# A graph-convolution kernel: zero rows behind h written first, x's other rows loaded in eight pieces on SyncE's queue, clearings begun five groups later

## The chip, the cores and the metric

The kernel runs on one core of one Trainium2 chip. The metric is the device time in microseconds of one execution; of several executions the median is taken.

## The reference: what is computed

A pre-normalised message-passing layer over 12,500 nodes and 400,000 edges, all in float32, with feature width 128 and 20 radial features per edge. The edges come sorted by `dst`.

```python
h = jnp.maximum(_layernorm(x, axis=-1), 0.0)           # [12500, 128]
h = h @ W_in2f.T
Wij = smu(f_ij @ W_f1.T + b_f1) @ W_f2.T + b_f2        # [400000, 128]
Wij = Wij * rcut_ij[:, None]
x_ij = h[idx_j] * Wij                                  # idx_j is dst (sorted)
agg = jax.ops.segment_sum(x_ij, idx_i, num_segments=h.shape[0])   # idx_i is src (any order)
out = smu(agg @ W_o1.T + b_o1) @ W_o2.T + b_o2
x = x + out
```

`smu` is a gelu-like bend with an erf in it.

## The kernel before, in words

**Tiles, groups, passes.** 128 edges are a tile, 4 tiles a group (512 edges), 8 tiles a super-tile (`SUP`, two groups). The 3,125 tiles are cut into nine passes (`PARTS`, called epochs in the code); the first has 59 super-tiles, that is 118 groups. For each group TensorE, ScalarE and VectorE make the messages: `hide` (L517) and `weigh` (L567) are the two filter products, `bend` (L525) and `smooth` (L533) the bend between them, `gather` (L548) takes the rows of h with a one-hot product, `take` (L556) copies them, `mix` (L577) multiplies, `turn` (L587) transposes back, and `send` writes the message tile `ms`: the row index within the bin by VectorE (L594), the four scaled copies by ScalarE (L597). Then GpSimd stores the four tiles with one indirect DMA each (L600) into DRAM buckets `buf{k}` of the pass, one bucket for each of the 98 bins of 128 nodes. Where a row goes is found by counting: `bins` (L438, L449, L452), `count` (L465, L466), `read` (L495), `number` (L504). While pass k makes messages, the buckets of pass k-1 are loaded (`fetch`, L631) and summed with one-hot products (`choose` L642, `add` L655). The fetch of a pass's buckets waits until all its stores have landed.

**Buckets must be cleared.** The tail of every bucket, from a guaranteed fill on, is set to zero by DMAs from the `zero` tile (`clear`, L167; 387 KB for two bins), issued by SyncE. For pass 0 they run in groups 0 to 37, spread evenly, and the constant `BY` (44 groups) is the point up to which the messages surely stay below the cleared region; later stores may wait for the clearings. From group `BY` on the clearings of pass 1 are issued, to the end of the pass.

**h and its windows.** The rows of h are needed by edges whose `dst` they are, and `dst` is sorted, so the first pass needs only the rows of the first 4 bins (`HEAD`). They are made before the loop; the other 94 bins are made during the first pass and stored in `h_dram` (L214). Each super-tile loads one window of 128 rows of `h_dram` at a row number that is read from SBUF (`window`, L415 and L416). Because that address is known only at run time, such a load is ordered against every write of `h_dram`, and every write against the loads before it. `N + WIN` rows exist; the ones behind the last bin must be zero. `zeroed` writes them (L731 to L733).

**The order of the work is written out by hand.** For TensorE, VectorE, ScalarE and SyncE the instruction order is the program's order; each works through its own in turn. The main loop over the groups (L776) first issues the loads of a later super-tile (`load`, L405 for the radial features, L407 for the relative indices, L416 for the window), then clearings, then the group's work. Three times in a group it calls `step()`: after `turn` and `send` of this group (the first slot), after `mix` of the next group (the second slot), and at the end (the third slot). `step()` takes from a list of side steps, `others()`, at an even pace: a step is taken while `taken_steps * 318 < slot * COUNT`, so at 276 steps nearly every slot takes one. The list is:

- the limits of chunk 0 and `zeroed`;
- for each of six further chunks of 512 tiles (`head_of`): `fetched` (SyncE asks for `dst` and `src`, 256 KB each, L301 and L302), `based` (VectorE's first use of `dst`, L305 to L307), `spread` (TensorE, L312), `lowered` (VectorE, L316), `turned` (TensorE, L321), `written` (ScalarE L327, then SyncE's store to `rel_dram`, L328), `binned`, `placed`, `limits`; after each of these nine one `stats` of a bin of x (L180, L181);
- the remaining `stats`, two in a step;
- `deviations`, and then 24 units of `rows_of_h` of six steps each: `normed` (VectorE, L191), `turned` (TensorE, L197), `cut` (ScalarE, L200), `product` (TensorE, L205), `first_part` (L208, L209), `other_parts` (L212, L213 and the store L214);
- `output_bias`.

**x.** x lives in the tile that later holds `agg`. Its first four bins are loaded at the start on ScalarE's queue. `late_loads` (L374) asks for the others on GpSimd's queue: three DMAs of 31 bins (L381, 1984 KB each) and one for the last bin (L382), then the rest of the edge weights (L384, 1306.5 KB) and small things. Small writes by VectorE (L376, L379) hold these DMAs back until that point.

**hs.** One tile `hs` (bufs=1) takes the three bf16 parts of h before they are stored, and serves as the buffer of `written` in the chunks after the first.

Of the kernel before, what the change touches and what calls it, by code (L numbers as in the profile page):

```python
# [9 lines left out]
F32 = mybir.dt.float32  # L10
# [9 lines left out]
P = 128  # L20
# [19 lines left out]
def gnn_kernel(  # L40
# [129 lines left out]


    HEAD = 4
    BY = 44
    x_sb = agg.rearrange("p (b d) -> p b d", d=D)
    mv = const.tile([P, NB, 2], F32, name="mv")
    rstd = const.tile([P, NB], F32, name="rstd")
# [84 lines left out]
    with tc.tile_pool(name="ld", bufs=4) as ld, \  # L261
# [14 lines left out]
        def fill(i):  # L276
            nc.vector.memset(fbufs[i], 1.0)

        hs = edge.tile([P, GRP, 3, D], BF, name="hs", bufs=1)
        early = eps_of[0][1] + 3  # L280

        def bank(name):
# [2 lines left out]
        def head_of(c):  # L285


            a, n = c * CH, min(CH, NT - c * CH)
            s0, m = a // SUP, (n + SUP - 1) // SUP
            rw = rowp.tile([P, ROWS, ROW], F32, name="rw").rearrange("p q r -> p (q r)")  # L290
            di, si, rel = rw[:, 0:n].bitcast(I32), rw[:, CH:CH + n].bitcast(I32), rw[:, 2 * CH:2 * CH + n]
            if c:
                rb = hs[:, :, 0, :]
            else:
                rb = edge.tile([P, SUP * P], BF, name="oh", bufs=3)[:, :CH].rearrange("p (j e) -> p j e", e=P)
            base_f = edge.tile([1, CH // SUP], F32, name="base_f")
            cells = [(j * P, min(P, n - j * P)) for j in range((n + P - 1) // P)]
            kept = [None]

            def fetched():  # L300
                nc.sync.dma_start(di, dst_col[:, a:a + n])  # L301
                nc.sync.dma_start(si, src_col[:, a:a + n])  # L302

            def based():
                nc.vector.tensor_copy(base_i[:, s0:s0 + m], di[0:1, 0:n:SUP])  # L305
                nc.vector.tensor_copy(base_f[:, :m], base_i[:, s0:s0 + m])
                nc.vector.tensor_copy(rel, di)  # L307

            def spread():
                pb = kept[0] = bank("pb")  # L310
                flat = pb.rearrange("p j e -> p (j e)")[:, :m * SUP].rearrange("p (s t) -> p s t", t=SUP)
                nc.tensor.matmul(flat, ones1, base_f[:, :m].unsqueeze(2).to_broadcast([1, m, SUP]),  # L312
                                 start=True, stop=True)

            def lowered():
                nc.vector.tensor_sub(rel, rel, kept[0].rearrange("p j e -> p (j e)")[:, :n])  # L316

            def turned():
                pd = kept[0] = bank("pd")
                for j, (o, w) in enumerate(cells):  # L320
                    nc.tensor.transpose(pd[:w, j, :], rel[:, o:o + w], ident)  # L321

            def written():
                w = cells[-1][1]
                whole = len(cells) - (w < P)
                if whole:
                    nc.scalar.activation(rb[:, :whole], kept[0][:, :whole], AF.Copy)  # L327
                    nc.sync.dma_start(rel_dram[0, a * P:(a + whole * P) * P].rearrange("(c t e) -> t c e", t=P, e=P),  # L328
                                      rb[:, :whole])
                if w < P:  # L330
                    nc.scalar.activation(rb[:w, whole], kept[0][:w, whole], AF.Copy)
                    nc.sync.dma_start(rel_dram[0, (a + whole * P) * P:(a + n) * P].rearrange("(t e) -> t e", e=P),
                                      rb[:w, whole])

            def limits():
                nc.vector.tensor_reduce(lh[:, 0, c:c + 1], rel, op=ALU.min, axis=AX.X)
                nc.vector.tensor_reduce(lh[:, 1, c:c + 1], rel, op=ALU.max, axis=AX.X)

            def bounded():
                most = edge.tile([1, 1], F32, name="most")  # L340
                nc.vector.tensor_reduce(most, base_f[:, :early], op=ALU.max, axis=AX.X)
                nc.vector.tensor_scalar(bad[0:1, 2:3], most, float(HEAD * P - WIN), None, op0=ALU.is_gt)
                nc.vector.tensor_scalar(base_i[:, :early], base_f[:, :early], float(HEAD * P - WIN), None, op0=ALU.min)

            def binned():
                nc.vector.tensor_scalar(di, si, 7, None, op0=ALU.arith_shift_right)
                nc.vector.tensor_copy(hi_b[:, a:a + n], di)

            def placed():
                nc.vector.tensor_scalar(di, si, P - 1, None, op0=ALU.bitwise_and)  # L350
                nc.vector.tensor_copy(lo_b[:, a:a + n], di)

            return dict(fetched=fetched, based=based, spread=spread, lowered=lowered, turned=turned, written=written,
                        limits=limits, bounded=bounded, binned=binned, placed=placed)
# [9 lines left out]
        nc.scalar.dma_start(w_f2, w_f2_t)  # L364
        nc.scalar.dma_start(b2, b_f2.rearrange("o p -> p o"))
        nc.scalar.dma_start(w_sb[:, 0:CH], w_col[:, 0:CH])
        for i in range(NF):
            fill(i)
        nc.vector.memset(zero, 0.0)
# [4 lines left out]
        def late_loads():  # L374

            nc.vector.memset(x_sb[:, NB - 1, :], 0.0)  # L376
            parts_of_x = chunks(NB - 1 - HEAD, 31)
            for a, n in parts_of_x:
                nc.vector.memset(x_sb[:, HEAD + a, 0:1], 0.0)  # L379
            for a, n in parts_of_x:  # L380
                nc.gpsimd.dma_start(x_sb[:, HEAD + a:HEAD + a + n, :], bin_rows(x, HEAD + a, n))  # L381
            nc.gpsimd.dma_start(x_sb[:LASTB, NB - 1, :], x[(NB - 1) * P:N, :])  # L382
            nc.vector.memset(w_sb[:, CH:CH + 1], 0.0)
            nc.gpsimd.dma_start(w_sb[:, CH:NT], w_col[:, CH:NT])  # L384
            nc.gpsimd.dma_start(w_o1, w_o1_t)
            nc.gpsimd.dma_start(w_o2, w_o2_t)
            nc.gpsimd.dma_start(b1, b_o1.rearrange("o p -> p o"))
            nc.gpsimd.dma_start(b2row, b_f2)
            nc.gpsimd.dma_start(bo2, b_o2.to_broadcast([P, P]))
# [305 lines left out]
            stats(edge, b)  # L695
        deviations(0, HEAD)
        rw = rowp.tile([P, ROWS, ROW], F32, name="rw")
        for step in rows_of_h(0, HEAD, *[rw[:, j * GRP:(j + 1) * GRP, 0:P] for j in range(3)], hs, bank):
            step()
        for s in range(3):  # L700
            window(s)
# [25 lines left out]
        cleared = at_first = done = 0  # L727
        work = []

        def zeroed():  # L730
            zr = edge.tile([P, 3 * D], BF, name="zr", bufs=1)  # L731
            nc.vector.memset(zr, 0.0)
            nc.sync.dma_start(h_dram[NB * P:N + WIN, :], zr[:N + WIN - NB * P, :])  # L733

        def output_bias():

            nc.vector.tensor_scalar(w_o2, w_o2, GC, None, op0=ALU.mult)
# [3 lines left out]
            nc.tensor.matmul(pb1, b1w, w_o2, start=True, stop=True)  # L741
            nc.vector.tensor_add(bo2, bo2, pb1)

        def others():
            yield one["limits"]
            yield zeroed
            left = list(range(HEAD, NB))
            for c in range(1, NC):
                it = head_of(c)
                for name in ("fetched", "based", "spread", "lowered", "turned", "written", "binned", "placed", "limits"):  # L750
                    yield it[name]
                    if left:
                        yield lambda b=left.pop(0): stats(edge, b)
            while left:
                two, left = left[:2], left[2:]
                yield lambda two=two: [stats(edge, b) for b in two]
            yield lambda: deviations(HEAD, NB)
            for b, n in chunks(NB - HEAD, GRP):
                rw = rowp.tile([P, ROWS, ROW], F32, name="rw")
                four = [rw[:, j * GRP:(j + 1) * GRP, 0:P] for j in range(3)]  # L760
                yield from rows_of_h(HEAD + b, n, *four, hs, bank)
            yield output_bias

        COUNT = 2 + 18 * (NC - 1) + (NB - HEAD - 9 * (NC - 1) + 1) // 2 + 1 + 6 * -(-(NB - HEAD) // GRP) + 1
        h_steps = others()
        taken_steps = slot = 0

        def step():

            nonlocal taken_steps, slot  # L770
            slot += 1
            while taken_steps < COUNT and taken_steps * 3 * (eps_of[0][1] * PER - 12) < slot * COUNT:
                next(h_steps)()
                taken_steps += 1

        for g in range(NG):  # L776
# [7 lines left out]
                cleared = 0  # L784
            if g < BY:

                while at_first < min(len(cleans) - 1, -(-(g + 1) * (len(cleans) - 1) // (BY - 6))):
                    apart(clear(0, at_first, nc.sync), "filled", "cleared")
                    at_first += 1
            elif k + 1 < EPOCHS:  # L790
# [34 lines left out]
            bins(g + 3)  # L825
            parts(k - 1, hi)
            step()
            assert k == 0 or taken_steps == COUNT and next(h_steps, None) is None
        k = EPOCHS - 1
        begin(k)  # L830
        choose(k, order_of[k][0])
# [222 lines left out]
```

## Time and profile before

| What | us |
|---|---|
| median of 3 runs (lowest, highest) | 4170.57 (4166.96, 4171.32) |
| profiled execution, device time | 4170.47 |
| its span, first to last instruction | 4168.6 |
| first indirect store begins | 32.87 |
| last store of the first pass begins (store 472 of 3125) | 668.62 |
| last indirect store begins | 4057.5 |

The profiled execution's device time lies 1.9 us above its span. The profile's page gives, for each engine, its busy time, and for groups of instructions the mean duration and the idle time of the engine just before them, with what ended most of it. In the timeline a row is: start in us, duration in us, engine, line, operation, output<-inputs, and in brackets the idle time before it with its releaser. An engine written with a q (SPq, POOLq) is the sequencer that issues DMAs. In the list of windows, each engine's busy time is followed by its instruction count in brackets; then come TensorE's granted clock (1.00 is full), the mean busy share of the 16 DMA engines, and GB/s.

### The profile page before, as it was taken

What the parts mean: (1) busy time and instruction counts of PE and PEld (TensorE: products, weight loads), DVE (VectorE), ACT (ScalarE), POOL (GpSimd) and SP (SyncE); (2) the same over time, 40 slices, a digit from 0 to 9 for tenths busy, and PEclk for the clock granted to TensorE, in tenths of its full rate; (3) what the DMA queues carried; (4) which work ended last, traced back from release to release, by engine and by line L of the source; (5) the groups of instructions that cost most, each with busy time, mean ns of one, the idle gap of its engine ahead of it and who ended that gap; (6) DMA issues with size and microseconds to landing.
All of it is one profiled execution on the core that took longest, in us unless ns stands there. A gap on an engine that the chain in (4) does not pass through costs nothing.

```text
span 4168.6 us, 74614 instructions
## 1 busy us (share of the span) xinstructions
PE 3724.3 (89%) x18497; PEld 2310.5 (55%) x18794; DVE 3202.9 (77%) x8556; ACT 2823.1 (68%) x11054; POOL 3055.0 (73%) x3169
## 2 busy tenths in 40 slices
PE   6877888999997999979999979999899899899898
PEld 2333434655554655545655546666566566556567
DVE  6886767877776877768877768888688788788777
ACT  5776777776766777657777657777677667677651
POOL 4777767777777777777777777777777777777762
PEclk9999999999999999999999999999999999999999
DMA  8955565766656766647666747777699699788667
GB/s 232 226 149 167 175 169 177 215 202 193 201 165 190 214 203 199 199 142 217 209 202 196 200 150 216 212 212 206 180 231 232 172 250 253 211 224 223 172 186 233
DMA packets 510408, 834.71 MB, mean 200 GB/s; under 512 B 84499, under 2 KB 322852, under 8 KB 509838
## 3 DMA queue, kind: packets, MB, share of 16 engines
q1 hardware_dynamic: 393900, 608.10, 53.0%
q0 software_dynamic: 101872, 214.27, 16.7%
q10 hardware_dynamic: 14194, 7.46, 0.6%
q8 instruction: 152, 2.49, 0.3%
q14 instruction: 290, 2.38, 0.2%
HBM read 456.16 MB, written 373.36 MB: 199 GB/s over the span
## 4 chain that ended last, share of the span: by engine, by line
PE 55%; DVE 20%; DMA 14%; ACT 7%; issue 3%; POOL 1%; DVEq 0%; SPq 0%; POOLq 0%; ACTq 0%
PE pw L567 13%; PE pg L655 13%; DMA buf<-ms,ix 12%; PE pu L517 10%; PE ph L548 8%; PE pt L587 6%; DVE se L642 5%; DVE mt L577 4%; DVE sm L533 3%; ACT ge L525 2%; ACT ms L597 2%; ACT jk L495 2%; DVE co L452 1%; DVE po L438 1%; DVE agg L668 1%
## 5 line engine op out<-in xcount | busy, mean ns | idle before, releaser
L600 POOL DMA_INDIRECT buf<-ms,ix x3125 | 3013.1, 964 | 1018.3 <-issue 264.5
L655 PEld LDWEIGHTS pg<-se,rw 128*128 128x128 f32 x8036 | 1088.8, 192 | 153.0 <-issue 14.8
L597 ACT ACTIVATE ms<-pt,w_sb 128x128 f32<-128x128 f32 x3125 | 902.5, 391 | 332.5 <-PE pt L587 181.8
L655 PE MATMUL pg<-se,rw 128*128 128x128 f32 x8036 | 1110.3, 276 | 7.8 <-DVE se L642 7.8
L495 ACT ACTIVATE jk<-pc,nbig 128x98 f32<-128x98 f32 x3125 | 1024.5, 350 | 2.7 <-PE pc L466 2.0
L567 PE MATMUL pw<-sm,w_f 128*128 128x512 f32 x1564 | 885.5, 649 | 41.5 <-DVE sm L533 36.2
L525 ACT ACTIVATE ge<-pu 128x512 f32<-128x512 f32 x782 | 467.9, 598 | 569.2 <-PE pu L517 546.4
L577 DVE SCALAR_TENSOR_TENSOR mt<-pw,b,hg 128x512 f32<-128x512 f32 x782 | 583.0, 745 | 346.8 <-ACT hg L556 345.9
L517 PE MATMUL pu<-f,w_f 128*128 128x512 f32 x1564 | 814.3, 603 | 5.4 <-DVE sm L533 5.4
L587 PE MATMUL pt<-ident,mt 128*128 128x128 f32 x3125 | 494.5, 281 | 293.7 <-DVE mt L577 290.3
L533 DVE SCALAR_TENSOR_TENSOR sm<-pu,ge 128x512 f32<-128x512 f32 x782 | 535.2, 684 | 215.3 <-ACT ge L525 206.4
L642 DVE TENSOR_TENSOR se<-irow_ps,rw 128x1536 f32<-128x1536 f32 (+1 forms) x345 | 587.5, 1703 | 146.9 <-DMA rw<-buf 127.5
L556 ACT ACTIVATE hg<-ph 128x512 f32<-128x512 f32 x782 | 468.7, 599 | 325.5 <-PE ph L548 323.5
L495 ACT ACTIVATION_READ_ACCUMULATOR jk<-pc,nbig 128x1 f32 x3125 | 674.3, 216 | 0.0
L548 PE MATMUL ph<-oh,hw 128*128 128x512 bf16 (+1 forms) x2049 | 631.7, 387 | 16.6 <-issue 0.7
L587 PEld LDWEIGHTS pt<-ident,mt 128*128 128x128 f32 x3125 | 353.3, 142 | 383.4 <-DVE mt L577 375.4
L452 DVE TENSOR_TENSOR co<-co,po 128x98 f16<-128x98 f16 x2353 | 501.8, 213 | 81.1
L548 PEld LDWEIGHTS <-hw 128*128 128x128 bf16 x2346 | 233.0, 99 | 555.3 <-issue 455.9
L438 DVE TENSOR_TENSOR po<-irow_ps,hi_b 128x392 f16<-128x392 f32 x782 | 433.3, 554 | 0.0
L567 PEld LDWEIGHTS pw<-sm,w_f 128*128 128x128 f32 x1564 | 238.0, 191 | 172.8 <-DVE sm L533 163.7
L517 PEld LDWEIGHTS pu<-f,w_f 128*128 128x128 f32 x1564 | 254.3, 196 | 29.6 <-DVE sm L533 7.0
L465 PE MATMUL pc<-co,ones_h 128*128 128x392 f16 x782 | 258.0, 330 | 1.0 <-ACT ms L597 1.0
(122 smaller groups left out, 1708.6 us busy)
## 6 DMA issues: line engine op xcount, KB each, us to landing
rw<-buf SPq DMA_DIRECT2D x292, 774.0 KB
rbc<-rel_dram SPq DMA_DIRECT2D x390, 256.0 KB
buf<-zero SPq DMA_DIRECT2D x243, 387.0 KB
buf<-ms,ix POOLq DMA_INDIRECT x3125
buf<-zero SPq DMA_DIRECT2D x193, 258.0 KB
hw<-h_dram SPq DMA_DIRECT2D x391, 96.0 KB
rw<-buf SPq DMA_DIRECT2D x49, 645.0 KB
f<-in_f_t SPq DMA_DIRECT2D x390, 80.0 KB
```

The costliest lines, as they stand in the source:

```text
L495: nc.scalar.activation(jk, pc[:, j], AF.Relu, bias=nbig, accum_out=sl[:, j:j + 1])
L517: nc.tensor.matmul(pu[:, :n], w_f1, loaded[g // PER][0][:, o:o + n], start=True, stop=True)
L525: nc.scalar.activation(ge[:, :n], units_of[g][:, :n], AF.Gelu, scale=ZS)
L533: nc.vector.scalar_tensor_tensor(sm[:, :n], units_of.pop(g)[:, :n], LIN, hidden[g][:, :n], op0=ALU.mult, op1=ALU.add)
L548: nc.tensor.matmul(ph[:, :n], hw[:, q * D:(q + 1) * D], oh[:, o:o + n], start=(q == 0), stop=(q == 2))
L567: nc.tensor.matmul(pw[:, :n], w_f2, hidden.pop(g)[:, :n], start=True, stop=True)
L577: nc.vector.scalar_tensor_tensor(mt[:, :n], pws.pop(g)[:, :n], b2, rows_of.pop(g)[:, :n], op0=ALU.add, op1=ALU.mult)
L587: nc.tensor.transpose(pt[:, j, :], mt[:, j * P:(j + 1) * P], ident)
L597: nc.scalar.activation(ms[:, j, 0:P], pt[:, j], AF.Copy, scale=w_sb[:, t + j:t + j + 1])
L600: i = nc.gpsimd.indirect_dma_start(out=bufs[k][:, :], out_offset=bass.IndirectOffsetOnAxis(ap=ix[:, j:j + 1], axis=0), in_=ms[:, j, :], in ...
L642: nc.vector.tensor_tensor(se[:, :m], irow_ps.unsqueeze(1).to_broadcast([P, m, P]), rows_in[c][:, :m, P:P + 1].to_broadcast([P, m, P]), op= ...
L655: nc.tensor.matmul(pgs[0][:, g, :], rows_in[c][:, o, 0:P], sel[c][:, o, :], start=(q == 0), stop=(q == Q[k] - 1))
```

## The change

Four edits:

1. The zero rows behind h are written at the very start: the memset of `zr` stands ahead of VectorE's first fills, and the DMA goes on ScalarE's queue, behind its first loads. The step `zeroed` is gone.
2. x's other rows leave `late_loads` (with the small writes that held them back) and become eight pieces of 12 bins (786 KB, the last 10 bins) on SyncE's queue. They are side steps: one right after the limits of chunk 0, one ahead of each of the six chunks, and the last after them. Chunk 1 has no `stats` between its steps any more; the others have them as before, and what remains is taken in pairs.
3. The clearings of pass 0 begin in group 6 instead of group 0, at the same rate (48 in 38 groups), and `BY` is 50 instead of 44, which also moves the start of pass 1's clearings.
4. `hs` becomes a tile taken anew for each use from a pool of two buffers. The side steps are a list instead of a generator; `COUNT` becomes 279.

```diff
-    BY = 44
+    BY = 50
...
-        hs = edge.tile([P, GRP, 3, D], BF, name="hs", bufs=1)
+        def parts_tile():
+            return edge.tile([P, GRP, 3, D], BF, name="hs")
+
...
-                rb = hs[:, :, 0, :]
+                rb = parts_tile()[:, :, 0, :]
...
         nc.scalar.dma_start(w_sb[:, 0:CH], w_col[:, 0:CH])
+        zr = edge.tile([P, 3 * D], BF, name="zr", bufs=1)
+        nc.vector.memset(zr, 0.0)
+        nc.scalar.dma_start(h_dram[NB * P:N + WIN, :], zr[:N + WIN - NB * P, :])
         for i in range(NF):
             fill(i)
...
             nc.vector.memset(x_sb[:, NB - 1, :], 0.0)
-            parts_of_x = chunks(NB - 1 - HEAD, 31)
-            for a, n in parts_of_x:
-                nc.vector.memset(x_sb[:, HEAD + a, 0:1], 0.0)
-            for a, n in parts_of_x:
-                nc.gpsimd.dma_start(x_sb[:, HEAD + a:HEAD + a + n, :], bin_rows(x, HEAD + a, n))
-            nc.gpsimd.dma_start(x_sb[:LASTB, NB - 1, :], x[(NB - 1) * P:N, :])
...
-        def zeroed():
-            zr = edge.tile([P, 3 * D], BF, name="zr", bufs=1)
-            nc.vector.memset(zr, 0.0)
-            nc.sync.dma_start(h_dram[NB * P:N + WIN, :], zr[:N + WIN - NB * P, :])
...
+        def old_piece(a, n):
+            for b, m in chunks(n, n if a + n < NB else n - 1):
+                if a + b < NB - 1:
+                    nc.sync.dma_start(x_sb[:, a + b:a + b + m, :], bin_rows(x, a + b, m))
+                else:
+                    nc.sync.dma_start(x_sb[:LASTB, NB - 1, :], x[(NB - 1) * P:N, :])
...
+        PIECE = 12
+        loads = [lambda a=a, n=n: old_piece(HEAD + a, n) for a, n in chunks(NB - HEAD, PIECE)]
+        single = [lambda b=b: stats(edge, b) for b in range(HEAD, NB)]
+        steps = [one["limits"], loads.pop(0)]
+        for c in range(1, NC):
+            mine = named(lambda c=c: head_of(c),
+                         ("fetched", "based", "spread", "lowered", "turned", "written", "binned", "placed", "limits"))
+            if loads:
+                steps.append(loads.pop(0))
+            for f in mine:
+                steps.append(f)
+                if c > 1:
+                    steps.append(single.pop(0))
+        steps += loads
+        for i in range(0, len(single), 2):
+            steps.append(lambda two=single[i:i + 2]: [f() for f in two])
+        steps.append(lambda: deviations(HEAD, NB))
+        units_of_rows = [named(lambda b=b, n=n: rows_unit(HEAD + b, n), range(6)) for b, n in chunks(NB - HEAD, GRP)]
+        for unit in units_of_rows:
+            steps += unit
+        steps.append(output_bias)
+        COUNT = len(steps)
...
-                while at_first < min(len(cleans) - 1, -(-(g + 1) * (len(cleans) - 1) // (BY - 6))):
+                while at_first < min(len(cleans) - 1, -(-(g - 5) * (len(cleans) - 1) // (BY - 12))):
                     apart(clear(0, at_first, nc.sync), "filled", "cleared")
```

`named` makes a unit's steps from its names and creates the unit's tiles when its first step is taken; `rows_unit` does that for one unit of `rows_of_h`.

More of the change, by code (lines that the diff above doesn't have):

```diff
@@ L697, in gnn_kernel @@
         rw = rowp.tile([P, ROWS, ROW], F32, name="rw")
-        for step in rows_of_h(0, HEAD, *[rw[:, j * GRP:(j + 1) * GRP, 0:P] for j in range(3)], hs, bank):
+        for step in rows_of_h(0, HEAD, *[rw[:, j * GRP:(j + 1) * GRP, 0:P] for j in range(3)], parts_tile(), bank):
             step()
@@ L742, in output_bias @@
             nc.vector.tensor_add(bo2, bo2, pb1)
[L744 to L762, printed above, removed]
@@ L764, in gnn_kernel, with named, run @@
-        COUNT = 2 + 18 * (NC - 1) + (NB - HEAD - 9 * (NC - 1) + 1) // 2 + 1 + 6 * -(-(NB - HEAD) // GRP) + 1
-        h_steps = others()
+        def named(make, names):
+            box = {}
+            def run(name, begin):
+                if begin:
+                    box.update(make())
+                box[name]()
+            return [lambda name=name, i=i: run(name, i == 0) for i, name in enumerate(names)]
+        def old_piece(a, n):
[4 more added lines that the diff above has]
+                    nc.sync.dma_start(x_sb[:LASTB, NB - 1, :], x[(NB - 1) * P:N, :])
@@ new lines, in rows_unit @@
+        def rows_unit(b, n):
+            rw = rowp.tile([P, ROWS, ROW], F32, name="rw")
+            four = [rw[:, j * GRP:(j + 1) * GRP, 0:P] for j in range(3)]
+            return dict(enumerate(rows_of_h(b, n, *four, parts_tile(), bank)))
+        PIECE = 12
[11 more added lines that the diff above has]
+                    steps.append(single.pop(0))
@@ L772, in step @@
             while taken_steps < COUNT and taken_steps * 3 * (eps_of[0][1] * PER - 12) < slot * COUNT:
-                next(h_steps)()
+                steps[taken_steps]()
                 taken_steps += 1
@@ L827, in gnn_kernel @@
             step()
-            assert k == 0 or taken_steps == COUNT and next(h_steps, None) is None
+            assert k == 0 or taken_steps == COUNT
         k = EPOCHS - 1
```

## The prediction

> **What bounds the kernel now.** I read the page first: which engine works at one pace from start to end? POOL is busy for 3055 us of 4168.6, nearly all of it in one line, the 3125 indirect stores.
>
> ```profile
> span 4168.6 us, 74614 instructions
> ...
> PE 3724.3 (89%) x18497; PEld 2310.5 (55%) x18794; DVE 3202.9 (77%) x8556; ACT 2823.1 (68%) x11054; POOL 3055.0 (73%) x3169
> ...
> L600 POOL DMA_INDIRECT buf<-ms,ix x3125 | 3013.1, 964 | 1018.3 <-issue 264.5
> ```
>
> One store is 0.96 us, with a gap of 0.30 us before the next, whatever the releaser named: 1.26 us, four to a group, so 5.05 us for a group of 512 edges. 3125 x 1.26 = 3938 us. The first store begins at 32.9 us and the last at 4057.5, so all other idle time of POOL is about 87 us. What is worth looking for is where POOL's gaps exceed 0.30. The timeline of POOL shows it at once:
>
> ```profile
> 36.76 0.96 POOL L600 DMA_INDIRECT buf<-ms,ix  x1 [0.30 <-issue]
> 42.27 0.96 POOL L600 DMA_INDIRECT buf<-ms,ix  x1 [4.55 <-ACT hg L556]
> 43.53 0.96 POOL L600 DMA_INDIRECT buf<-ms,ix  x1 [0.30 <-ACT jk L495]
> 49.84 0.96 POOL L600 DMA_INDIRECT buf<-ms,ix  x1 [5.34 <-DMA agg<-in_x]
> 53.65 0.96 POOL L600 DMA_INDIRECT buf<-ms,ix  x1 [2.86 <-DMA w_sb<-in_w_col]
> 58.71 0.96 POOL L600 DMA_INDIRECT buf<-ms,ix  x1 [4.11 <-DVE ix L504]
> ...
> 66.45 0.96 POOL L600 DMA_INDIRECT buf<-ms,ix  x1 [3.00 <-ACT hg L556]
> ...
> 536.54 0.95 POOL L600 DMA_INDIRECT buf<-ms,ix  x1 [3.62 <-ACT hs L208]
> ...
> 613.84 0.96 POOL L600 DMA_INDIRECT buf<-ms,ix  x1 [0.72 <-ACT hg L556]
> ```
>
> To see who is late, I set each group's first store beside the moment the group is ready (the later of its four ACT copies L597 and its DVE copy L594). Groups 1, 2, 3: ready at 41.5, 58.0, 65.7, stored 0.75 us later: compute is late. From 4 to 85 groups wait for POOL, up to 21.6 us (group 42). From 86 to 107 the store again follows readiness by 0.75 us (ready at 494.8 and 613.1): while the rows of h are made compute falls to 5.66 us a group and is the bound. From 108 POOL is. The first pass ends with POOL's last store, on which the fetch of the buckets hangs; the chain of waits has it there:
>
> ```profile
> 668.62 2.27 DMA buf<-ms,ix
> 670.90 5.40 DMA rw<-buf
> ```
>
> So the pass ends at ready(107) + 0.75 + 11 x 5.07, and an early gain of compute reaches it one for one. Later passes run at 1.27 us a store; they are moved, not changed.
>
> Why compute is late at 42 to 66 us: the timelines of DVE and SP, and the windows of 10 us (columns: sum, PE, PEld, DVE, ACT, POOL, clock, DMA share, GB/s).
>
> ```profile
> 54.80 0.21 DVE L305 COPY base_i<-rw 1x64 int32<-1x64 int32 x1 [11.84 <-DMA rw<-in_dst_col]
> ...
> 122.88 0.27 DVE L305 COPY base_i<-rw 1x64 int32<-1x64 int32 x1 [2.69 <-DMA rw<-in_dst_col]
> ```
> ```profile
> 40.74 0.39 SPq L733 DMA_DIRECT2D h_dram<-zr  x1
> 41.17 0.36 SPq L301 DMA_DIRECT2D rw<-in_dst_col  x1
> ```
> ```profile
> 50.00:60.00 10.00, 4.72 (x6) 1.45 (x7) 3.05 (x13) 0.00 (x0) 2.73 (x4) 0.50 1.05 301
> ```
>
> DVE stands 11.84 us at L305 for the indices of chunk 1. SP asks for them only at 41.17, because the write of the zero rows in front of them (L733) waits for window reads of h_dram (12.0 us in two waits); then they share full DMA engines with x, asked for in one go at 21 us.
>
> **What the Trainium skill says.** "DMA: Bandwidth & Descriptors", section "Issuing engines are not separate DMA queues": DMAs of all issuers run on the same 16 engines. The trace agrees: share 1.05 at 50 to 60 us, x from POOL beside SP's loads; moving x to SP makes it no cheaper. "TensorE: Matmul & The Clock Gate", section "Part 1: The HAM clock gate": an idle TensorE falls to half clock. It agrees: clock 0.50 in that window, and L567 takes 2.00 us for its pair against 1.12. So a wait costs more than its length. "VectorE: DVE Perf Modes", section "Zero memsets can be issued as uint32": one cycle per element; the zr memset runs as 192 uint32 in 0.22 us.
>
> **The change, part by part.** Edits of no time: the step list in place of a generator; the second hs tile (no wait for hs's store shows among ACT's waits in the h rows; without that cover, under 1 us a row unit).
>
> 1. Zero rows first. Added ahead of DVE's first fills, which run back to back into L305 of chunk 0 (7.32 us): +0.22. Its store on ACT's queue (0.4 us) lies before a table load at 7.8 that nothing needs before 11.8: nothing; if it were needed, 0.4. Removed: L733 and its wait on SP.
>
> 2. x in pieces. By the step rule (steps taken x 318 < slots x COUNT, three slots a group, COUNT 276 to 279) pieces 0 and 1 fall in group 0, chunk 1's request in group 1's first slot, its use (L305) in that group's second, after L577. No zero write stands before them and SP has nothing to wait for (it stood ready at 27.7 us), so the request goes out near 29 us. Ahead or beside are 1.6 MB of x, 1.3 MB of w_sb, 0.5 MB of indices and about 1 MB of small loads from 20 us on: 4.4 MB at the 301 GB/s above is 15 us, landed by 36 to 40. DVE gets there at 42.2. The 11.84 us go. So do POOL's waits of 5.34 and 2.86, for the x loads and w_sb ahead in POOL's queue. Worth: groups 2 and 3 took 65.7 - 41.5 = 24.2 us; the next five took 4.40 each (65.7 to 87.7); 24.2 - 8.8 = **-15.4**. POOL follows: group 3 stored at 52.4 instead of 66.45, 14.05 earlier. Group 1's own 4.55 stays, being the first groups' latency.
>
> 3. Chunks 2 to 6. Each index load now has a piece of x (786 KB) before it in SP's queue: 2.0 us at 396 GB/s (window 40 to 50 us) to 3.2 at 243 (80 to 90 us, share 1.08); I take 2.7. Before, chunk 3 was 2.69 us late; by SP's timeline and bytes the others had about 4, 3, 1 and 5 us to spare. Afterwards: chunk 2 has no clearings before it (they begin in group 6), no wait. Chunk 3 has four groups from the write of chunk 2 to its use, as before, but some five clearings against four and a piece more: late by about 5.3. Chunks 4 and 5 get 0.67 of a group (3 us) more: even. The wait of 2.69 cost 5.6 (groups 16 and 17 took 14.8, two of 4.6 are 9.2): half is the cold TensorE, paid once. So 2.6 more: **+2.6**; ends: -5.6 (no wait) and +26 (rival 3).
>
> 4. Clearings later: 48 of 387 KB, still 1.26 a group, now groups 6 to 43; those of the next pass have 64 groups instead of 70, +9% at a DMA share of 0.6: nothing, at worst 1 us. The stats that chunk 1 no longer carries come back as five more pairs: 9 x 0.46 us moved, sum zero.
>
> 5. Slots shift. In the h rows, a transpose in a group's first slot right after the norming in the last slot before makes TensorE wait for DVE: six such groups took 7.7 us on average, the others 5.4. By the step rule they are seven afterwards: **+2.3**; counting all neighbourhoods of steps instead gives +4.7, luck in the alignment -3.
>
> Sum: +0.2 - 15.4 + 2.6 + 2.3 = -10.3. The profiled execution took 4170.47 us (span 4168.6 and 1.9 around it), 0.1 under the median of the three runs, 4170.57. 4170.5 - 10.3 = 4160.2, so 4160.
>
> **Rivals.**
> Rival 1, larger: indices never late again. For: chunks 2 and 3 meet fewer clearings. -15.4 - 5.6 + 0.2 = -20.8, but compute can run only six ms tiles ahead of POOL: 6 x 5.07, less 4.7 for the four stores of a group and 2.3 for landing, is 23.4 against 21.6 reached, so 1.8 beyond POOL's own 14 to 16: -16 to -18. 4153.5.
> Rival 2, hidden: the early gain is given back, by chunk 3 late by twice my figure and the +4.7: -15.4 + 0.2 + 5.3 + 4.7 = -5. 4165 to 4170. Against: the h rows' sum is as likely to be smaller.
> Rival 3, slower: x before every index load. With 3.2 us of x and 2 us more of clearings before each, chunks 2 to 5 are late by 1, 8, 2.4 and 4.2: 15 us of waits, times 2.1 (5.6/2.69) 32, less 5.6 already paid, 26; -15.4 + 26 = +10.8: 4181. It decides when L305's waits pass (15.4 + 5.6)/2.1 = 10 us in all. For: 0.90 to 1.08 DMA share at 80 to 200 us. Against: SP stands some 10 us at each chunk's write (L328), in which the queues drain.
> That the change doesn't do what it says: if the pieces on SP had to wait for DVE's reads of x's tile, SP would lose its lead; that too ends in rival 3's waits. The separate waits of x's parts before speak against it.
>
> **Numbers.** Mine 0.45, own range 4155 to 4165 (0.33 faster, 0.12 not); rival 1 0.27; rival 2 0.13; rival 3 0.15. What a measurement of this kernel can tell from no change is about 0.2%, 8.3 us, so 4162.2. Faster 0.33 + 0.27 = 0.60, same 0.25, slower 0.15. The range: down to 4147 (rival 1 with good alignment, 3 in 100 below), up to 4174, above which most of rival 3 lies (12 in 100); about 15 in 100 are left out.
>
> **What would show it.** Right: no L305 wait in chunk 1, group 3 stored near 52 us, POOL's gaps 0.30 from there; one L305 wait, in chunk 3, near 5 us; ready(107) near 603; the last store of the pass near 658. Wrong: L305 waits over 10 us in sum; gaps in POOL before 400 us; h-row groups off 5.7 us; later passes not simply shifted.

## The result, and the profile after

The changed kernel takes 4185.46 us (median of 7, 4179.85 to 4191.62) where the kernel before takes 4170.57 on the same chip: ratio 1.0037, 95% interval 1.0025 to 1.0048. It is slower by 15 us; forecast was 4160. The profiled execution took 4189.22 us. Thirteen of the runs told below were made where every kernel, the one before too, took 5225 to 5306 us (called the slower chips below, though one chip number of the record, 2, stands on both sides); their times stand against the kernel before in the same session, and little is built on them.

The page of the changed kernel, the lines that answer to those of before:

```profile
span 4187.4 us, 74904 instructions
...
PE 3736.3 (89%) x18794; PEld 2306.4 (55%) x18794; DVE 3201.5 (76%) x8553; ACT 2835.9 (68%) x11054; POOL 3057.7 (73%) x3165
...
L599 POOL DMA_INDIRECT buf<-ms,ix x3125 | 3022.0, 967 | 1035.2 <-issue 262.9
```

The shares are the same; POOL's idle time before its stores went from 1018 to 1035 us, and a mean store from 964 to 967 ns. The timeline of POOL shows what the change was made for:

```profile
42.31 0.96 POOL L599 DMA_INDIRECT buf<-ms,ix  x1 [4.07 <-ACT hg L555]
...
47.47 0.96 POOL L599 DMA_INDIRECT buf<-ms,ix  x1 [0.30 <-ACT hg L555]
...
52.53 0.96 POOL L599 DMA_INDIRECT buf<-ms,ix  x1 [0.30 <-issue]
```

The gaps of 5.34, 2.86, 4.11 and 3.00 are gone, and group 3 is stored at 52.53 instead of 66.45. Yet the first pass ends later: its last store begins at 677.95, before at 668.62. SP asks for its buckets at 680.40, before at 670.90:

```profile
680.40 2.21 SPq L630 DMA_DIRECT2D rw<-buf  x4
```

Set beside each other group by group, the moments at which a group is ready differ from before by -14.4 us at group 3, -12.8 at group 12, then -4.8 at 13, -2.9 at 15, -8.8 at 20, -2.7 at 21 and +0.2 at 23; they stay within 2 us of zero up to group 48 and go to +9.2 at group 80, +8.8 at 104. So the gain came, was lost in two places (groups 13 to 23 and 48 to 80), and these are what the experiments are about. DVE's waits for the columns, as the `dst` indices of a chunk are called from here on, in the first 320 us (sum, number, longest), and the timeline of the same line (L307 is the L305 of before, the first use of a chunk's columns) name the first place:

```profile
DVE base_i L307 <- DMA rw<-in_dst_col: 14.5, 3, 7.1
```
```profile
104.54 0.20 DVE L307 COPY base_i<-rw 1x64 int32<-1x64 int32 x1 [7.11 <-DMA rw<-in_dst_col]
...
144.75 0.20 DVE L307 COPY base_i<-rw 1x64 int32<-1x64 int32 x1 [6.23 <-DMA rw<-in_dst_col]
```

No wait in chunk 1, but 7.11 us in chunk 3 and 6.23 in chunk 4 (1.2 in a third). TensorE's waits in the first 700 us name the second place:

```profile
PE pg L197 <- DVE rw L191: 34.0, 21, 4.7
```

`turned` waits for `normed` of the h rows 34.0 us in sum; before it was 28.1. The longest case shows why a place costs so much (DVE, changed kernel):

```profile
291.53 0.74 DVE L185 RECIPROCAL rstd<-rstd 128x94 f32<-128x94 f32 x1 [0.76 <-ACT rstd L184]
293.44 0.69 DVE L532 SCALAR_TENSOR_TENSOR sm<-pu,ge 128x512 f32<-128x512 f32 x1 [1.17 <-ACT ge L524]
...
295.83 1.10 DVE L191 TENSOR_SCALAR rw<-agg,mv,rstd 128x128 f32<-128x128 f32 x4
```

DVE does `deviations` and most of a group's work before L191, and TensorE's next instruction in its own order is the transpose of these rows.

### The profile page after: what moved, and what is told of

The parts are those of the page before. It is cut to its first block, busy times and chain, and to the rows that moved or that the text cites. A ratio compares the mean times of both kernels' runs of the same rounds, so it can differ in the third digit from the quotient of the medians.

```text
span 4187.4 us, 74904 instructions
## 1 busy us (share of the span) xinstructions
PE 3736.3 (89%) x18794; PEld 2306.4 (55%) x18794; DVE 3201.5 (76%) x8553; ACT 2835.9 (68%) x11054; POOL 3057.7 (73%) x3165
## 4 chain that ended last, share of the span: by engine, by line
PE 49%; DVE 15%; DMA 12%; ACT 5%; issue 3%; POOL 0%; DVEq 0%; ACTq 0%; POOLq 0%; SPq 0%
PE pg L654 13%; DMA buf<-ms,ix 12%; PE pw L566 12%; PE pu L516 8%; PE ph L547 7%; PE pt L586 6%; DVE se L641 5%; DVE mt L576 3%; DVE sm L532 2%; ACT ge L524 2%; DVE agg L667 1%; ACT ms L596 1%; PE pc L464 1%; PE pc L465 1%; DVE po L437 1%
## 5 line engine op out<-in xcount | busy, mean ns | idle before, releaser
L654 PEld LDWEIGHTS pg<-se,rw 128*128 128x128 f32 x8036 | 1086.6, 192 | 152.8 <-issue 14.2
L547 PE MATMUL ph<-oh,hw 128*128 128x512 bf16 x2346 | 648.6, 386 | 1.7 <-DVE ix L503 1.7
```

Of the source, the lines that this page charges most:

```text
L547: nc.tensor.matmul(ph[:, :n], hw[:, q * D:(q + 1) * D], oh[:, o:o + n], start=(q == 0), stop=(q == 2))
L654: nc.tensor.matmul(pgs[0][:, g, :], rows_in[c][:, o, 0:P], sel[c][:, o, :], start=(q == 0), stop=(q == Q[k] - 1))
```

## The experiments

Line numbers are each kernel's own. All ratios are against the kernel before on the same chip. "Control" is the kernel before, run again (c0); its group times are what the others are set against.

### The two kernels again

> The kernel before, unchanged, as a control on the same chip. In the first pair of profiles every store on POOL took 3 ns longer after the change (1.266 us from store to store against 1.263), and VectorE's and ScalarE's instructions 1 to 2 ns more. Theory A (chips differ in their clock): here the kernel before shows the pitch of the chip, and the kernel after on the same chip shows the same one. Theory B (the change makes a store longer): 1.263 here, 1.266 in the kernel after. Ratio 1.000 in either case.

Measured: 4165.59 us, ratio 1.0000 [0.9991, 1.0008]. Its chunk 1 waits 12.0 us as before, but the wait of 2.69 in chunk 3 isn't there, and its first pass ends 4.8 us sooner than in the first profile of before (663.84): a wait that comes or stays away from execution to execution. In the first profile the last completion notice of that DMA came at 122.85, 3.3 us after the one recorded ahead of it.

> The changed kernel, unchanged, for a profile on the same chip as the control. Theory A: same store pitch as the control, the last store of the first pass 7 to 9 us later than the control's, later passes equal within 3 us; ratio 1.002 to 1.003. Theory B: pitch 3 ns longer, so 8 us more over the later passes; ratio 1.004 to 1.005.

Measured: 4176.18 us, ratio 1.0029 [1.0018, 1.0040]. L307 waits 5.19 us in chunk 3 and 6.04 in chunk 4; group 3 is ready 14.2 us ahead of the control, group 12 12.8 ahead, group 23 4.0 behind, group 48 2.1, group 80 8.9 behind. Pass 1 ends 9.7 later. A store takes 958 ns in the median of both profiles, so the 961 of the first profile after isn't the change's doing; about 9.7 of the 10.6 us between the medians is there at the end of pass 1.

### e1: each piece of x behind the chunk's columns

```diff
-            if loads:
-                steps.append(loads.pop(0))
-            for f in mine:
+            for i, f in enumerate(mine):
                 steps.append(f)
+                if i == 0 and loads:
+                    steps.append(loads.pop(0))
```

> Each piece of x is asked for right behind its chunk's indices instead of ahead of them. Theory 'the piece delays the indices': VectorE's waits for dst in the chunks (14.5 us in three) fall to under 4 us, ready times of groups 25 to 45 come 10 to 13 us earlier than in the changed kernel, and the pass ends 8 to 12 us earlier: ratio to the kernel before 1.000 to 1.001. Rival 'the clearings ahead of the indices are what delays them': the waits stay over 10 us and the ratio stays 1.003 to 1.004.

Measured: 4166.39 us, ratio 1.0005 [0.9997, 1.0014]. DVE's waits:

```profile
DVE base_i L307 <- DMA rw<-in_dst_col: 0.5, 1, 0.5
```

Group 24 is 11.3 us ahead of the control (changed kernel: 3.1 behind), group 48 5.0 ahead, group 80 1.6 behind; pass 1 ends 2.6 later. So the first loss is this wait: mended, it takes 7.1 us off the end. It doesn't take off the full 14.4 of group 24, because the lead shrinks on its own from 11.9 us (group 34) to 5.0 (48), and then the second loss follows as in c1 (6.7 us from group 48 to 80, there 6.8).

Why are the columns late? SP's timelines, the changed kernel (c1), e1, and the control with its use of these columns:

```profile
83.79 0.62 SPq L751 DMA_DIRECT2D agg<-in_x  x1
84.50 2.74 SPq L404 DMA_DIRECT2D f<-in_f_t  x1
...
89.11 2.07 SPq L167 DMA_DIRECT2D buf<-zero  x2
91.22 1.15 SPq L303 DMA_DIRECT2D rw<-in_dst_col  x1
```
```profile
84.82 0.94 SPq L167 DMA_DIRECT2D buf<-zero  x2
85.81 0.95 SPq L303 DMA_DIRECT2D rw<-in_dst_col  x1
```
```profile
110.95 0.47 SPq L301 DMA_DIRECT2D rw<-in_dst_col  x1
...
119.75 0.19 DVE L305 COPY base_i<-rw 1x64 int32<-1x64 int32 x1
```

The columns are asked for 5.4 us later than in e1. A wait is the landing time less the lead that SP has on DVE. Landing is counted from the request to the last completion notice of the DMA in the trace, the lead from the request to the moment when DVE would use the columns.

| chunk | kernel | lead, us | landing, us | wait, us |
|---|---|---|---|---|
| 3 | control | 8.8 | 8.5 | 0 |
| 3 | c1 | 5.7 | 10.9 | 5.2 |
| 3 | e1 | 12.8 | 9.0 | 0 |
| 4 | control | 11.4 | 7.7 | 0 |
| 4 | c1 | 5.3 | 11.3 | 6.0 |
| 4 | e1 | 10.1 | 7.9 | 0 |

Both have moved. The landing grew by 2.4 and 3.7 us, about what a piece was priced at by its bytes, and the lead fell by 3.1 and 6.1. Some of what took the lead is in the rows: the piece's own request (0.62), and the request right behind a piece, which is held 2.74 us (L404, the load of the radial features, took 0.33 to 1.33 us in the other groups from 76 to 142 us, of this kernel and of before). In chunk 4 the piece's request took 1.31 and two clearings behind it 3.33 (0.94 in e1's row above); by an estimate from these figures that is 3.7 of the 6.1 us. The places of the steps have a part too: by the step rule the changed kernel uses the columns of chunk 3 two slots after asking for them, where the kernel before left three (chunk 4: two and two), and e1 leaves three and four. So e1 shows that the waits are the loss, but it changes the order on SP's queue and the distance to the use at once.

### e2: the steps' places

```diff
-        for i in range(0, len(single), 2):
-            steps.append(lambda two=single[i:i + 2]: [f() for f in two])
+        while single:
+            n = 3 if len(single) > 34 else 2
+            several, single = single[:n], single[n:]
+            steps.append(lambda several=several: [f() for f in several])
```

That makes 276 steps, as before the change, so that the h rows' steps fall into the slots that they had.

> The changed kernel with the stats behind the chunks taken in 22 steps instead of 25 (five threes and 17 pairs), so that there are 276 steps and every step of the h rows falls in the same slot as in the kernel before. Theory 'the slots' alignment costs the 8.6 us that compute lost between groups 48 and 88': from group 50 on the ready times no longer fall behind the kernel before; the pass ends 6 to 9 us earlier than in the changed kernel, ratio to the kernel before 1.001 to 1.002. Rival 'it is SyncE or the DMA traffic of the denser clearings in the h rows': still 6 to 9 us lost between groups 48 and 88, ratio 1.003 to 1.004.

Measured: 4171.09 us, ratio 1.0017 [1.0010, 1.0023]. TensorE's waits (c1: 33.8 us in 21, the longest 4.7):

```profile
PE pg L197 <- DVE rw L191: 27.9, 20, 2.7
```

From group 48 to 80 it needs 179.5 us; the control 181.9, c1 188.7. Groups over 6.8 us apart, from 44 to 107: 10 in c1, 6 here, 7 in the control. L307 still waits 10.0 us, in four. Pass 1 ends 2.4 us after the control's, 7.3 before c1's. So the second loss is the slots' alignment: the clearings stand where c1 has them, and the loss is gone. The time is 5.5 us over before though pass 1 accounts for 2.4; its profiled execution has stores of 962 ns against 958, and the rest of the difference stays open.

e2 also says something on the first loss. It has the order of c1, a piece ahead of the columns, and only other places, and its waits move: 3.5, 0.4, 2.5 and 3.7 us in chunks 3 to 6, where c1 has 5.2, 6.0, 0.1 and none. In chunk 4 the columns go out right behind the piece:

```profile
122.61 0.50 SPq L751 DMA_DIRECT2D agg<-in_x  x1
123.16 2.90 SPq L303 DMA_DIRECT2D rw<-in_dst_col  x1
```

They land 13.4 us after the request, later than for any other of chunks 2 to 6 in the profiles shown here, and yet DVE waits only 0.4, since its use comes 13.0 us after the request (c1: 5.3). So a piece right ahead of the columns need not make a wait where the lead is long enough.

### e3: both

The edits of e1 and e2 together.

> The changed kernel with each piece of x asked for right behind the chunk's index columns, and 276 steps as before the change. Two separate losses that add up: no L307 wait above 1 us in chunks 2 to 6 and no loss in groups 50 to 80; the lead of 11 us at group 24 falls to some 5 at group 44 by the waits for the six transposed tiles and then stays, pass 1 ends 3 to 8 us before the control's, ratio 0.998 to 0.9995. Rival, one loss that only shows at different places: the end of pass 1 is within 2 us of the control's as with each mending alone, ratio 1.0000 to 1.0010.

Measured: 4157.80 us, before 4161.53 on that chip: ratio 0.9991 [0.9983, 1.0000]. No L307 wait, 181.4 us from group 48 to 80, group 107 ready at 603.0, pass 1 ends at 659.27, 4.6 us before the control's. The two losses add up: 9.7 - 7.1 - 7.3 = -4.7, and -4.6 came. The control's profile is of another chip of the same speed, and its kernel's own pass ends lie 4.8 us apart, so the sum may fit better than it can; the ratios, 1.0029 - 0.0024 - 0.0012 = 0.9993, say the same.

| kernel | waits for `dst`, us | group 48 to 80, us | pass 1's last store against the control | ratio |
|---|---|---|---|---|
| control | 12.0 (chunk 1) | 181.9 | 0 | 1.0000 |
| changed (c1) | 11.2 | 188.7 | +9.7 | 1.0029 |
| e1 | 0.5 | 188.5 | +2.6 | 1.0005 |
| e2 | 10.0 | 179.5 | +2.4 | 1.0017 |
| e3 | none | 181.4 | -4.6 | 0.9991 |

It had stored group 3 12.7 us early and group 24 still 12.4. Where did the other 8 us go? From group 34 to 44 its groups' readiness falls from 12.9 to 6.0 us ahead, while POOL stays 11 us ahead. ACT waits for a free `ms` tile in that stretch, in the control as well (190 to 310 us, the control, then e3; DVE adds 1.6 us in e3 and nothing in the control):

```profile
ACT ms L597 <- DMA buf<-ms,ix: 3.6, 3, 2.0
```
```profile
ACT ms L596 <- DMA buf<-ms,ix: 4.4, 3, 1.9
```

Messages can't run further ahead of POOL than the six tiles hold, and a tile is free only when its stores have landed. A group's last store comes at most 22.9 us after its readiness in e3 (group 38; e1 23.4 at 39; c1, which is late, 17.4), but 25.3 in the control (group 40). So the limit is tighter in e3. For groups 34 to 37 the last data packets of a store end 4.6 us after its start in e3, in the mean, and 2.4 in the control. The DMA engines are full in e3 when these stores run (control, then e3; the last but one column is their share):

```profile
220.00:230.00 10.00, 8.83 (x33) 3.88 (x32) 8.16 (x32) 8.67 (x34) 7.56 (x9) 1.00 0.18 61
```
```profile
220.00:230.00 10.00, 8.71 (x32) 3.65 (x30) 8.54 (x38) 6.18 (x25) 7.57 (x9) 1.00 1.08 297
```

From 214 to 227 us SP asks for six clearings and the last piece of x in e3, for neither in the control. That the later clearings and the last pieces make the tiles scarce is thus argued from the traces; no run takes them out by themselves. POOL's own lead stays near 11 us up to group 72, then the h rows make compute the bound again, and there compute's lead is only 6: POOL's falls to 5.0 by group 84.

The same kernel ran three times on the slower chips: 5252.84 us, 1.0031 [1.0006, 1.0056]; 5292.66, 1.0022 [1.0002, 1.0041]; 5305.83, 1.0033 [1.0006, 1.0059]. There it is 0.2 to 0.3% slower than before. Compute bounds these chips, not POOL: a group's last store follows its readiness by 4.5 us in the median of pass 1, and by 7.9 at most (control above: 11.9, and up to 25.3). Why it loses there was not found. Their expectation:

> Both of the last edits together: the piece of x behind its chunk's indices, and 276 steps, so that the h rows' steps fall in the slots of the kernel before. Theory 'two separate losses, late indices (11 us) and alignment (6 us)': the early gain of 11 us is kept to the end of the pass except for what the six message tiles cap; the pass ends 4 to 8 us before the control's, ratio 0.998 to 0.999. Rival 'the losses overlap, because compute that is ahead is held by the message tiles and falls back to the same point': ratio 1.000 to 1.001, as with the piece behind alone.

### e4 and e7: is it the order on SP's queue?

e4 asks for the piece in the step of `fetched`, behind the columns, with an empty step where it was; e7 asks for the pieces in their own slots, but on ACT's queue (the line for the last rows, not shown, is changed alike).

```diff
+            piece = loads.pop(0) if loads else None
+            if piece:
+                steps.append(lambda: None)
...
+                    steps.append(lambda f=f, piece=piece: (f(), piece()))
```
```diff
-                    nc.sync.dma_start(x_sb[:, a + b:a + b + m, :], bin_rows(x, a + b, m))
+                    nc.scalar.dma_start(x_sb[:, a + b:a + b + m, :], bin_rows(x, a + b, m))
```

> The changed kernel with an empty step where the piece of x stood, and the piece issued in the same step right behind the chunk's indices: every step keeps its slot, only the order of the two requests on SyncE's queue differs. Theory 'the piece ahead delays the indices, by its bytes (2.7 us) and by SyncE's next requests that are held 2.7 to 3.4 us behind it': VectorE's waits for dst fall from 11.2 us to 0 to 3, ratio 1.000 to 1.001. Rival 'what helped before was the slot, which brought the request ahead of group 12's loads and clearings': waits of 6 us or more remain, ratio 1.002 to 1.003.

> The changed kernel with the pieces of x asked for on ACT's queue, in the same steps. If the columns are late because they are queued behind the piece on SP: L307 waits under 2 us, group 24 some 10 us ahead of the control, ratio 0.9995 to 1.0015 (ACT pays some us for the requests, which may show as waits for hg or ge). If the bytes of x in flight make them late whichever queue asks: L307 waits of 7 to 14 us as in the changed kernel, ratio 1.0025 to 1.0035.

Measured, all on the slower chips: e4 5230.64 us, 1.0006 [0.9984, 1.0029]; again 5289.56, 1.0027 [1.0011, 1.0043]; again 5297.05, 1.0008 [0.9988, 1.0029]. e7 5301.10, 1.0019 [0.9999, 1.0039]. No L307 wait in any. But at these chips' pace DVE comes 11.7 to 12.5 us after the request of chunk 3, and in c1 the columns landed in about 11: the wait could hardly have shown. These runs tell nothing on the order, and e8, e7 with 276 steps (5305.48, 1.0017 [0.9996, 1.0038]), tells nothing on the sum:

> The kernel with the pieces on ACT's queue and 276 steps as before the change. If the order on SP's queue and the places of the normalizing steps are the two losses and add up: pass 1 ends 3 to 8 us before the control's, ratio 0.998 to 0.9995, as for the pieces behind the columns with 276 steps. If only one of them is real: ratio 1.0000 to 1.0015.

### e5 and e6: one part of the change alone

e5 is the kernel before with the zero rows written first (the step `zeroed` left empty), e6 is it with the later clearings (`BY = 50`, and the new rate) and nothing else.

```diff
         def zeroed():
-            zr = edge.tile([P, 3 * D], BF, name="zr", bufs=1)
-            nc.vector.memset(zr, 0.0)
-            nc.sync.dma_start(h_dram[NB * P:N + WIN, :], zr[:N + WIN - NB * P, :])
+            pass
```
```diff
-    BY = 44
+    BY = 50
...
-                while at_first < min(len(cleans) - 1, -(-(g + 1) * (len(cleans) - 1) // (BY - 6))):
+                while at_first < min(len(cleans) - 1, -(-(g - 5) * (len(cleans) - 1) // (BY - 12))):
```

> The kernel before with the zero rows alone moved to the start (an empty step in their place); x stays on GpSimd's queue, clearings from group 0. Theory 'SyncE's wait ahead of the request was most of the 11.9 us': the indices of chunk 1 are asked for near 30 us instead of 41, and VectorE waits 3 us or less; ready(3) 8 to 12 us earlier; but POOL stays held by the x loads in its own queue (waits of 5 and 3 us near 45 to 55 us). Ratio 0.998 to 0.999. Rival 'x on full DMA engines was most of it': the request goes out early but the indices land near 50 us, VectorE waits 7 us or more, ratio 0.9985 to 1.000.

> The kernel before with the clearings alone moved (groups 6 to 43, BY 50). Theory 'clearings are no cause': the wait of chunk 1 shortens by 2 to 4 us (six fewer clearings by then), the 9% more clearings per group in the h rows cost under 1 us; ratio 0.999 to 1.0005. Rival 'the denser clearings in the h rows cost what compute lost there': compute loses 4 us or more between groups 50 and 88; ratio 1.001 or more.

Measured on the slower chips: e5 5238.31, 1.0010 [0.9985, 1.0034], again 5274.18, 0.9997 [0.9976, 1.0019]; e6 5234.97, 0.9982 [0.9955, 1.0008], again 5278.07, 1.0007 [0.9986, 1.0029]. Neither is told from no change. The first 60 us of e5's second run say something all the same (SP, DVE), beside e6, which has the zero rows where they were:

```profile
29.87 0.35 SPq L301 DMA_DIRECT2D rw<-in_dst_col  x1
...
52.78 0.20 DVE L305 COPY base_i<-rw 1x64 int32<-1x64 int32 x1 [7.75 <-DMA rw<-in_dst_col]
```
```profile
41.36 0.34 SPq L301 DMA_DIRECT2D rw<-in_dst_col  x1
...
51.96 0.20 DVE L305 COPY base_i<-rw 1x64 int32<-1x64 int32 x1 [8.22 <-DMA rw<-in_dst_col]
```

Asked for 11.5 us sooner, the columns land no sooner: 22.9 us instead of 10.6 in transit. So the zero rows alone didn't hold chunk 1; x, asked for in one go at 21 us, is the rival that is left. No run moves x alone: with the zero rows where they were, columns asked for at 41 could still have come after DVE.

### e9: eight message tiles

e8 with eight `ms` tiles and ten `ix` tiles.

```diff
-            tc.tile_pool(name="msg", bufs=6) as msg, \
+            tc.tile_pool(name="msg", bufs=8) as msg, \
...
-            ix = cnt.tile([P, GRP], I32, name="ix", bufs=8)
+            ix = cnt.tile([P, GRP], I32, name="ix", bufs=10)
```

> The changed kernel with the pieces of x on ACT's queue in the change's own slots, 276 steps as before the change, eight ms tiles in place of six (and ten ix tiles in place of eight). If the order on SP's queue made the columns late: L307 waits under 2 us in sum; if x's bytes in flight did: 5 to 12 us as in the changed kernel. If the six tiles take the rest of the lead: no ms wait on the stores' landing, the lag from a group's readiness to its last store passes 26 us, and pass 1 ends 9 to 13 us before the control's with the L307 waits gone (4152 to 4157 against a before of 4162 to 4166, ratio 0.9970 to 0.9985), 2 to 6 us with them there. If the tiles aren't it: pass 1 ends 3 to 6 us before the control's, ratio 0.9985 to 0.9995.

Measured: 5228.97 us, 0.9997 [0.9968, 1.0026], again on a slower chip, where no group gets more than 7.7 us ahead of its last store. Whether eight tiles keep the lead is not known. That the six take it in e3 rests on the waits and the lags above.

## Why the prediction was wrong, step by step

1. **Zero rows first, +0.22: right** (L307 of chunk 0 at 7.5 instead of 7.3 us), but by itself of no use. I had named the zero write as a cause of chunk 1's wait; without it, and with x as before, the wait was hardly shorter (e5, on a slower chip: 7.75 us, e6 8.22).
2. **x in pieces, -15.4: right.** Ready(3) moved by 14.4 and its store by 13.9 (forecast 14.05; 52.4 forecast, 52.53 measured). The columns of chunk 1, asked for at 29.41, were there when DVE came at 42.9.
3. **Chunks 2 to 6, +2.6: this step failed.** I priced a piece by its bytes, 2.7 us ahead of the columns, and let SP keep its lead on DVE. The bytes came about as priced: the landing grew by 2.4 and 3.7 us. The lead, put at no loss at all, fell by 3.1 and 6.1 us, by the request that is held behind a piece and by the places of the steps. The wait in chunk 3 was sized well (5.3; measured 7.1 and 5.2), in part by luck, since it was built on a wait of 2.69 that the control doesn't have; chunk 4 was called even and waited 6.2 and 6.0. From group 12 to 23 the changed kernel lost 13.0 us against the profile before, where +2.6 stood, and 16.8 against the control (c1), where it would have been 8.2, the 5.6 for the wait of 2.69 included. Each us of wait cost 1.5 (16.8 for 11.2), where I had taken 2.1. At the end of pass 1 e1 gets 7.1 us of it back, the rest being lost later in any case (6).
4. **Clearings later, nothing: not settled.** Nothing was seen in e6, on chips that would show only some 10 us and in whose traces of e6 nothing waits for a message tile. In e3 the later clearings lie where the lead is lost.
5. **Slots, +2.3, up to +4.7: right in kind, three times too small:** 7.3 us (e2). L197's waits make 5.9 of it (34.0 against 28.1; 33.8 against 27.9). I counted the places where `turned` follows `normed` at once, but not `deviations` ahead of one (4.7 us for one wait).
6. **"An early gain of compute reaches it one for one" failed too.** With both losses mended, 12.7 us at group 3 became 4.6 at the end. Rival 1 reckoned with the six tiles, but as a cap of 23.4 us on the wait for a group's first store, above the 21.6 of before, which would have let POOL's lead through. Measured, that wait reached 19.1 us in e3 and 19.6 in e1, less than the control's 21.5. Its 2.3 us for the landing of a store is the figure that doesn't hold there: with the 4.6 us of e3 the same sum gives 21.1.

The sum with measured sizes: -12.7 (group 3, e3) + 8.1 (what e3 loses after it) + 7.1 + 7.3 = +9.8 where -10.3 stood; 9.7 came. The 8.1 is a remainder, so the sum tests only that the two losses add up. Rival 3, with the right sign at 0.15, named the waits and their turning point: L305 waits over 10 us in sum make the change slower. They were 14.5 and 11.2, and it was. Its price, 4181, lies 4.5 us under the first measurement. Its cause, the bytes of x and of clearings, is half of what the table of e1 shows; it too left the lead as it was. My argument against it, that SP stands 10 us at each chunk's write while the queues drain, didn't apply: the piece, its follower and the columns all go out in one stretch after that stand.

Two readings in the prediction are slightly off and change nothing: groups 86 to 107 take 5.63 us each, not 5.66, and L567's pair in the idle window takes 2.08 us, not 2.00.

Left open: how the lost lead splits between the held request and the places of the steps (e1 changes both, e2 the places alone); what tightens the limit of the six tiles; what the slower chips do to the kernels with pieces; and, in the changed kernel, the 1 to 6 us of the medians that lie behind pass 1.

## What to carry to other kernels

When a load is cut into pieces that go out ahead of time-critical small loads, compute the lead that the small request keeps on its user (request to use, in the profile before). Set against it both the longer landing and what the issuing queue loses behind each piece, and count the steps that are left between request and use; put the small request first. Where side steps are handed out by an even pace, a change in their count moves all later ones against the main work: keep the count, or check which producer now stands right before its consumer. Ahead of calling an early gain a gain at the end, ask how far the stage may run ahead of the bound engine.

## What the runs showed of the hardware

- A request on SP right behind a piece of x (1536 rows of 512 bytes) is held in most cases: 3.29 us for the columns of chunk 1 (0.36 in the profile before), 2.72 and 2.74 for L404, 4.80 and 3.33 for two clearings, 4.87 for one (e1), but only 0.78 for the columns of chunk 2. In the profile before no request on SP took over 1.33 us in the first 230 us.
- The columns of a chunk (256 KB) landed 7.3 to 8.5 us after the request in the control (chunks 3 to 6) and 10.2 to 11.7 in c1, where each has a piece of x ahead of it.
- With the pieces spread, the DMA engines stand nearly idle where x had filled them, and are full later. Windows of the changed kernel (share is the last but one column; at 40 to 50 us it was 1.04 before):

```profile
40.00:50.00 10.00, 8.67 (x34) 3.94 (x34) 7.64 (x25) 7.54 (x32) 5.86 (x6) 1.00 0.11 34
...
60.00:70.00 10.00, 8.80 (x31) 3.66 (x30) 7.83 (x29) 7.22 (x30) 7.68 (x8) 1.00 1.07 279
```

  A piece or two more in that hole might take them from the chunks that wait; it wasn't tried.
- `deviations` costs ACT two table loads of 1.28 us around one instruction, and the bend of the next group waits for them (ACT, changed kernel):

```profile
289.21 0.60 ACT L555 ACTIVATE hg<-ph 128x512 f32<-128x512 f32 x1 [1.01 <-PE ph L547]
289.82 1.28 ACT L184 ACT_TABLE_LOAD   x1
291.12 0.38 ACT L184 ACTIVATE rstd<-mv,eps 128x94 f32<-128x94 f32 x1
291.52 1.28 ACT L524 ACT_TABLE_LOAD   x1
292.81 0.60 ACT L524 ACTIVATE ge<-pu 128x512 f32<-128x512 f32 x1
```

  The Trainium skill, "ScalarE: Activation LUTs", section "What ACT_TABLE_LOAD costs", gives 1283 ns for the load and 1380 ns more for a drain. The load agrees; of the drain nothing shows here: from the end of one instruction to the start of the next there are 1.31 us.
